# Causal self attention in fp32: in the third and fourth query blocks, four key blocks of a unit are turned by VectorE in 32x32 blocks and moved through DRAM, and their values come last

## The chip, the cores and the metric

The kernel runs on one core of one Trainium2 chip. The metric is the device time of one execution in microseconds. The engines are named as the profile names them: PE is TensorE (PEld its weight loads), DVE VectorE, ACT ScalarE, POOL GpSimd, and SP the engine whose queue issues every DMA of this kernel. Each works through its own instructions in program order; semaphores join them.

## What is computed

An encoder layer over 77 context tokens and a decoder layer over 2 batches of 2048 tokens, width 512, 16 heads of 32, all in fp32. The change is in the decoder's causal self attention:

```python
def _mha(xq, xkv, w_in, b_in, w_out, b_out, bias):
    ...
    scores = jnp.einsum('bhqd,bhkd->bhqk', q, k) / jnp.sqrt(jnp.asarray(hd, xq.dtype))
    scores = scores + bias[None]
    attn = jax.nn.softmax(scores, axis=-1)
    out = jnp.einsum('bhqk,bhkd->bhqd', attn, v)
    out = out.transpose(0, 2, 1, 3).reshape(Bq, Tq, D)
    return out @ w_out.T + b_out
...
causal = jnp.where(jnp.arange(Tt)[None, :] > jnp.arange(Tt)[:, None], -jnp.inf, 0.0)
sb = _rel_bias(dec_rel_self, Tt, Tt) + causal[None]
...
y = y + _mha(yn, yn, dec_sa_in_w, dec_sa_in_b, dec_sa_out_w, dec_sa_out_b, sb)
```

The relative bias is constant beyond 127 tokens, so that only the two key blocks nearest the diagonal need a bias added; a constant for all the other blocks drops out of the softmax.

## The kernel before, in words

The 2048 queries of a batch are four blocks (m = 0 to 3) of 512, each of four tiles (t) of 128. A **unit** (L329) is one batch, block, group g of four heads, and tile: 128 queries by i + 1 = 4m + t + 1 key blocks of 128 by four heads. There are 128 units; the 32 units with m = 2 have 9 to 12 key blocks, and the 32 with m = 3 have 13 to 16. The prediction calls these third-block and fourth-block units. pieces (L315) cuts a unit's key blocks into pieces of at most four.

A unit goes through these steps.

- **scores** (L357): for a piece, four matmuls (L375), one for each head, into four PSUM banks. VectorE evicts each into pp (L384), the SBUF buffer of scores and probabilities, and keeps the maximum; the last piece's two near blocks get their bias on the way (L391). With the unit's last piece VectorE forms nm, the negated maximum (L401). The four exponentials (L406, one for each head, in place, with the sum) are put into a list, late_exps, and issued by ScalarE later (exps, L352).
- **turn** (L412): the values product needs keys on partitions, and pp has queries there. So each 128x128 block of probabilities is transposed by TensorE against the identity (L427): a key block's four heads fill one PSUM bank, a "load", and ScalarE (L434) or VectorE (L432) copies it to a tile of pts. Of eight loads VectorE copies the fifth and the seventh, of fewer the second half.
- **values** (L441): for each key block four matmuls, one for each head, into the four 32-row strips of one bank (L456). The bank is copied to oT (L469), or added to it by VectorE (L471) for a second visit of the unit.

pp holds two units: even units lie at its start, odd ones at its end (probabilities, L344), so that unit n + 2 takes the places of unit n. The eight PSUM banks go round in a ring (bank, L180).

The order around these steps is written out in the loop at L1893. A unit is visited once for each pair of its pieces. A visit issues turn, then (in a unit's last visit) the **slot** of the next unit (L1324: projections, output products, and products of later stages that fill TensorE, with their weight loads into three wqk buffers), then one or two pieces of scores of later units as soon as their places in pp are free (may_score, L1857, score_two, L1873), then values, then more scores. The stream of pieces (L330) runs in order of units and of key blocks.

Softmax sums are inverted, sent through DRAM by SP (rec, rirows: L487, L492) and multiplied into oT by POOL (L494) a slot or two later. SP also loads the bias tiles (L341), the residual rows xr (L262), and the weights (L199, L1038, L1118), and stores y (L1106). A DMA that has to wait holds up all that stand behind it on SP.

## Time and profile before

| What | Time |
|---|---|
| three timed runs | 2726.55, 2729.14, 2731.93 us; median 2729.14 us |
| profiled execution, span from its first to its last instruction | 2726.8 us |
| TensorE busy in that span | 2708.1 us |
| VectorE, ScalarE, GpSimd busy | 1839.9, 1537.0, 1002.4 us |
| DMA, mean of the span | 141 GB/s |

The profile gives the profiled execution's time as its span; what lies around the span is not shown apart, and the span lies within the three runs. Its lines read so: engine, line of the code and operation, output tile <- input tiles, partitions x elements, count; then busy time and mean duration, and the time that the engine stood idle just before these instructions, with what ended most of it. In answers in order of time the first two numbers are start and duration in microseconds, and the idle time before stands in brackets. An fp32 product of scores or values leaves two matmul records, a transpose one.

### The profile page before, as it was taken

How to read it: one execution, taken by the hardware profiler on the slowest of the kernel's cores; microseconds unless marked ns; L12 is line 12 of the kernel's file. 1: busy time of each engine (PE TensorE's matmuls, PEld its weight loads, DVE VectorE, ACT ScalarE, POOL GpSimd, SP SyncE). 2: the span in 40 equal slices, each digit the busy share in tenths (PEclk: the TensorE clock that was granted, in tenths of full speed). 3: DMA queues.
4: the chain of work that ended last, by engine and by line, in shares of the span. 5: the costliest groups of instructions: out<-in, count | busy, mean ns of one | idle time of the engine just before them, and what ended most of it. 6: DMA issues, size and time to landing. Idle time of an engine off the chain costs nothing.

```text
span 2726.8 us, 68267 instructions
## 1 busy us (share of the span) xinstructions
PE 2708.1 (99%) x26606; PEld 2217.9 (81%) x26606; DVE 1839.9 (67%) x5445; ACT 1537.0 (56%) x2978; POOL 1002.4 (37%) x844
## 2 busy tenths in 40 slices
PE   9999999999999999999999999999999999999998
PEld 6678877777876677777777777898989898989898
DVE  4776688888885677788888783646464746464645
ACT  3554567777786547667777784444444444444431
POOL 2612235500300513322300203455556565656456
PEclk9999999999999999999999999999999999999999
DMA  8724355511213522343311206565657565656465
GB/s 242 213 92 135 126 155 164 168 50 43 67 45 89 143 76 72 111 133 98 126 50 35 79 19 220 171 214 173 213 171 239 168 216 170 218 166 219 151 224 185
DMA packets 296277, 385.10 MB, mean 141 GB/s; under 512 B 41184, under 2 KB 165648, under 8 KB 295826
## 3 DMA queue, kind: packets, MB, share of 16 engines
q1 hardware_dynamic: 295954, 380.73, 44.1%
q8 instruction: 211, 3.46, 0.5%
q14 instruction: 112, 0.92, 0.1%
HBM read 334.15 MB, written 46.47 MB: 140 GB/s over the span
## 4 chain that ended last, share of the span: by engine, by line
PE 95%; DVE 1%; ACT 1%; DMA 1%; POOL 1%; issue 1%; SPq 0%; DVEq 0%; POOLq 0%; ACTq 0%
PE psum L427 18%; PE psum L1638 14%; PE psum L1667 13%; PE psum L375 11%; PE psum L456 9%; PE psum L1134 8%; PE psum L1801 3%; PE psum L1758 3%; PE psum L1049 3%; PE psum L866 2%; PE psum L836 1%; PE psum L874 1%; PE psum L590 1%; PE psum L811 1%; PE psum L239 1%; PE psum L215 1%
## 5 line engine op out<-in xcount | busy, mean ns | idle before, releaser
L406 ACT ACTIVATE pp<-pp,nm 128x128 f32<-128x128 f32 (+15 forms) x512 | 611.8, 1200 | 28.6 <-DVE nm L401 27.8
L384 DVE TENSOR_SCALAR_CACHE_REDUCE pp<-psum 128x512 f32<-128x512 f32 (+3 forms) x1024 | 556.2, 591 | 51.3 <-PE psum L375 49.7
L434 ACT COPY pts<-psum 128x512 f32<-128x512 f32 x714 | 384.1, 594 | 312.6 <-PE psum L427 265.6
L427 PE MATMUL psum<-ident,pp 128*128 128x128 f32 x4352 | 530.4, 277 | 4.7 <-ACT nT L310 4.0
L427 PEld LDWEIGHTS psum<-ident,pp 128*128 128x128 f32 x4352 | 474.0, 141 | 55.7 <-DVE pp L384 21.4
L375 PE MATMUL psum<-kT,q 32*128 32x512 f32 (+3 forms) x2560 | 336.5, 559 | 2.5 <-DVE q L217 1.0
L456 PEld LDWEIGHTS psum<-pts,vv 128*32 128x32 f32 x8704 | 226.4, 110 | 127.4 <-DVE pp L384 55.4
L1667 PE MATMUL psum<-pp 128*128 128x128 f32 x2560 | 304.5, 276 | 1.9 <-POOL pp L962 1.6
L1667 PEld LDWEIGHTS psum<-pp 128*128 128x128 f32 x2560 | 296.3, 192 | 8.6 <-issue 2.8
L432 DVE COPY pts<-psum 128x512 f32<-128x512 f32 x374 | 245.2, 685 | 82.6 <-PE psum L427 80.3
L456 PE MATMUL psum<-pts,vv 128*32 128x128 f32 x8704 | 279.6, 276 | 0.8 <-DVE mx L391 0.3
L962 POOL TENSOR_TENSOR pp<-pp 128x512 f32<-128x512 f32 x159 | 212.8, 1356 | 111.0 <-DMA pp<-in_dec_ff_wT_dram 50.6
L1638 PE MATMUL psum<-vv,pp 128*128 128x256 f32 x1024 | 236.2, 381 | 0.0
L375 PEld LDWEIGHTS psum<-kT,q 32*128 32x128 f32 x2560 | 146.3, 183 | 107.1 <-issue 41.3
L1638 PEld LDWEIGHTS psum<-vv,pp 128*128 128x128 f32 x1024 | 190.3, 190 | 25.8 <-issue 0.5
L391 DVE CUSTOM_DVE_ANT_0 pp<-psum,bias 128x256 f32<-128x256 f32 (+1 forms) x512 | 196.0, 411 | 19.7 <-PE psum L375 19.7
L1651 DVE TENSOR_TENSOR kT<-kT,psum 128x512 f32<-128x512 f32 x96 | 65.8, 686 | 191.6 <-PE psum L1638 191.4
L1654 ACT ACTIVATE kT<-kT,vecs 128x256 f32<-128x256 f32 x192 | 86.9, 501 | 156.6 <-DVE kT L1651 155.9
L1638 PE MATMUL psum<-nT,pp 128*128 128x256 f32 x768 | 174.1, 380 | 0.5 <-DVE oT L471 0.5
L1638 PEld LDWEIGHTS psum<-nT,pp 128*128 128x128 f32 x768 | 144.2, 190 | 20.8 <-issue 1.4
L1675 ACT COPY oT<-psum 128x128 f32<-128x128 f32 x56 | 15.0, 268 | 238.9 <-PE psum L1667 238.9
L494 POOL TENSOR_TENSOR oT<-rirows,oT 128x512 f32<-128x512 f32 x30 | 38.4, 1280 | 293.6 <-DMA rirows<-rec 181.7
(272 smaller groups left out, 4110.6 us busy)
## 6 DMA issues: line engine op xcount, KB each, us to landing
pp<-w_d SPq DMA_DIRECT2D x520, 256.0 KB
pp<-in_dec_ff_wT_dram SPq DMA_DIRECT2D x112, 256.0 KB
bias<-tzg SPq DMA_DIRECT2D x128, 128.0 KB
pp<-wo_d SPq DMA_DIRECT2D x56, 256.0 KB
wqk<-in_dec_sa_in_wT_dram SPq DMA_DIRECT2D x52, 256.0 KB
wqk<-sa_q SPq DMA_DIRECT2D x84, 128.0 KB
vv<-in_enc_ff_wT_dram SPq DMA_DIRECT2D x8, 1024.0 KB
xr<-in_x_dram SPq DMA_DIRECT2D x32, 256.0 KB
```

The source lines that it names most:

```text
L375: nc.tensor.matmul(banks[r][:, : kn * P], q[rows4(r), ts(t, P)], kT[rows4(r), g, k0 * P : (k0 + kn) * P], start=True, stop=True,)
L384: nc.vector.tensor_scalar(p[:, k0 : k0 + far], s[:, :far], 1.0, None, ALU.mult, ALU.max, accum_out=st["mx"][:, r, c : c + 1],)
L391: nc.vector.tensor_tensor_reduce(p[:, k0 + far : i + 1], s[:, far:kn], near[:, 2 - (kn - far) :], 1.0, LOWEST, ALU.add, ALU.max, accum_out ...
L406: nc.scalar.activation(p, p, AF.Exp, bias=nm, accum_out=to)
L427: nc.tensor.transpose(pt[:, ts(x, P)], state[n]["p"][r][:, k], ident)
L432: nc.vector.tensor_copy(pts[:, : len(load), :], pt[:, :w])
L434: nc.scalar.copy(pts[:, : len(load), :], pt[:, :w])
L456: nc.tensor.matmul(ot[rows4(r)], vv[:, k, ts(g * HC + r, HD)], got.pop((n, k, r)), start=k == k0 and (whole or not begun), stop=k == k1 - ...
L962: engine.tensor_tensor(out, a, b, ALU.subtract)
L1134: nc.tensor.matmul(mm[:, ts(f, TOK)], left[:, c, ts(f, P)], right[:, c, :], start=c == 0, stop=c == 1,)
L1638: nc.tensor.matmul(mm[:, ts(f, TOK)], a[:, c, ts(f, P)], b[:, c, :], start=fresh and f == 0 and c == 0, stop=c == 1, skip_group_check=True,)
L1667: nc.tensor.matmul(psum[:, bank_i, ts(col, P)], lhs[:, c, :], w[:, c, :], start=fresh and k in (0, 3) and c == 0, stop=c == 3, skip_group_ ...
```

## The change

The first piece of four key blocks (0 to 3, the **far** blocks) of every unit with m = 2 or 3, but for the last two units of all, 62 units together, isn't transposed by TensorE any more.

- Their scores are evicted into pp in another order: within the unit's region of 2048 columns, a 32-key part a of each block, then head, then key block, then the 32 keys. The exponentials are as before.
- At the start of the unit's first visit, move(n) turns the region in place with two VectorE instructions of 128x1024, each of which transposes 32x32 blocks. After each of them SP stores that half (512 KB) to a DRAM tile, turn. Then SP loads the four quarters back, each to 32 partitions (256 KB). Each load waits for both stores.
- The far values are the last products of the unit's last visit. They read the region directly, as the moving operand in four runs of 32 columns, with no copy to pts.
- The pieces of a unit are scored in the order in which they are visited: the far piece last. A place in pp is free once its piece was transposed or, for the far piece, once the far values are issued (held_by, leave). The next user of the region, the far scores of unit n + 2, thus follows unit n's far values.
- A first visit has one piece where m = 2 and two where m = 3; the last visit has the rest.

VectorE in a third-block unit with 12 key blocks, from the sum into oT of the unit before to the inverse of the softmax sums; pp are the probabilities, pts the transposed ones, mx and nm the maxima. Before:

```order
L401 TENSOR_REDUCE nm<-mx 128x4
L471 TENSOR_TENSOR oT<-psum,oT 128x128
L432 COPY pts<-psum 128x512 x2
L384 TENSOR_SCALAR pp,mx<-psum 128x4x128 x8
L432 COPY pts<-psum 128x512 x2
L482 RECIPROCAL ri_109<-sums 128x16
```

The same place now:

```order
L515 TENSOR_TENSOR oT<-psum,oT 128x128
L421 TENSOR_SCALAR pp,mx<-psum 128x4x128 x4
L438 TENSOR_REDUCE nm<-mx 128x4
L385 STREAM_TRANSPOSE pp<-pp 128x1024 x2
L469 COPY pts<-psum 128x512 x2
L421 TENSOR_SCALAR pp,mx<-psum 128x4x128 x4
L469 COPY pts<-psum 128x512 x2
L526 RECIPROCAL ri_111<-sums 128x16
```

The four evictions of the far scores now stand ahead of nm, nm ahead of the two turnings, and these ahead of the copies of the pieces that TensorE still transposes.

TensorE in a fourth-block unit with 15 key blocks, from its first turn; vv are the values, nT and xt operands of the slot. Before:

```order
L427 MATMUL psum<-ident,pp 128x128 x32
L375 MATMUL psum<-kT,q 128x512 x8
L456 MATMUL psum<-pts,vv 32x128 x32
L427 MATMUL psum<-ident,pp 128x128 x28
L1049 MATMUL psum<-nT,wqk 128x256 x2
L1049 MATMUL psum<-xt,wqk 128x256 x2
L375 MATMUL psum<-kT,q 128x256 x4
L375 MATMUL psum<-kT,q 128x384 x4
L456 MATMUL psum<-pts,vv 32x128 x28
L427 MATMUL psum<-ident,pp 128x128 x32
```

The same place now:

```order
L464 MATMUL psum<-ident,pp 128x128 x32
L408 MATMUL psum<-kT,q 128x384 x4
L408 MATMUL psum<-kT,q 128x512 x4
L499 MATMUL psum<-pts,vv 32x128 x32
L464 MATMUL psum<-ident,pp 128x128 x12
L1093 MATMUL psum<-nT,wqk 128x256 x2
L1093 MATMUL psum<-xt,wqk 128x256 x2
L408 MATMUL psum<-kT,q 128x256 x4
L499 MATMUL psum<-pts,vv 32x128 x12
L499 MATMUL psum<-pp,vv 32x128 x16
L408 MATMUL psum<-kT,q 128x512 x4
L464 MATMUL psum<-ident,pp 128x128 x32
```

Sixteen transposes are gone from the second turn, the far values (those from pp) stand at the end, and the far scores of a later unit stand behind them, ahead of the next unit's first turn.

SP in two units of batch 0's fourth block, from the bias loads; xr are residual rows, y the stored result, turn the DRAM tiles. Before:

```order
L341 DMA bias<-tzg_76 32x4x256 x4
L199 DMA wqk<-in_dec_sa_in_wT_dram 128x4x128
L262 DMA xr<-in_x_dram 128x512 x2
L1106 DMA y_0_2_79<-xr 128x512 x2
L492 DMA rirows<-rec_114 32x512 x4
```

The same place now:

```order
L355 DMA bias<-tzg_76 32x4x256 x4
L199 DMA wqk<-in_dec_sa_in_wT_dram 128x4x128
L262 DMA xr<-in_x_dram 128x512 x2
L386 DMA turn_109<-pp 128x2x512 x2
L388 DMA pp<-turn_109 32x4x512 x4
L1150 DMA y_0_2_79<-xr 128x512 x2
L536 DMA rirows<-rec_116 32x512 x4
L386 DMA turn_110<-pp 128x2x512 x2
L388 DMA pp<-turn_110 32x4x512 x4
L199 DMA wqk<-in_dec_sa_in_wT_dram 128x4x128
```

Each unit puts two stores and four loads into SP's queue, between the loads and stores of the slots.

The diff, cut to its core:

```diff
         units = [(b, m, g, t) for b in range(B) for m in range(NMB) for g in range(NC) for t in range(TB)]
-        stream = [(n, k0, kn) for n, u in enumerate(units) for k0, kn in pieces(u[1] * TB + u[3])]
+
+        def moved(n):
+
+            return units[n][1] >= 2 and n < len(units) - 2
+
+        def visits_of(n):
+
+            ps = pieces(units[n][1] * TB + units[n][3])
+            if not moved(n):
+                return [(ps[v : v + 2], []) for v in range(0, len(ps), 2)]
+            far, *ps = ps
+            first = 2 if units[n][1] == NMB - 1 else 1
+            return [(ps[:first], []), (ps[first:], [far])]
+
+        stream = [(n, *p) for n in range(len(units)) for v in visits_of(n) for p in v[0] + v[1]]
         state = {}
         biases = {}
 
...
 
             for _ in range(min(k, len(late_exps))):
                 late_exps.pop(0)[1]()
+
+        bounce = [dram.tile([RB // 8, P, HC * P], F32, name=f"turn{k}", tag=f"turn{k}") for k in range(2)]
+
+        def region(n):
+
+            w = (units[n][1] + 1) * MB
+            at = END - HC * w if n % 2 else 0
+            return pp[:, at : at + HC * MB]
+
+        def move(n):
+
+            area = region(n).rearrange("p (a c) -> p a c", a=HC)
+            to = bounce[n // 2 % 2]
+            for a in (0, 2):
+                two = region(n)[:, a * HC * P : (a + 2) * HC * P]
+                nc.vector.transpose(two, two)
+                nc.sync.dma_start(to[a : a + 2].rearrange("a p c -> p a c"), area[:, a : a + 2])
+            for a in range(HC):
+                nc.sync.dma_start(area[rows4(a)], to[a].rearrange("(a q) c -> q a c", q=RB))
 
         def scores(n, k0, kn):
             b, m, g, t = units[n]
...
             for r in range(HC):
                 p, s, c = st["p"][r], banks[r].rearrange("p (k x) -> p k x", x=P), col
                 if far:
+                    to, got_s = p[:, k0 : k0 + far], s[:, :far]
+                    if k0 == 0 and moved(n):
+                        to = to.rearrange("p a (k x) -> p a k x", x=RB)
+                        got_s = got_s.rearrange("p k (a x) -> p a k x", x=RB)
                     nc.vector.tensor_scalar(
-                        p[:, k0 : k0 + far], s[:, :far], 1.0, None, ALU.mult, ALU.max,
+                        to, got_s, 1.0, None, ALU.mult, ALU.max,
                         accum_out=st["mx"][:, r, c : c + 1],
                     )
                     c += 1
...
 
         sums_held = {}
 
-        def values(pair):
-            n, k0, _ = pair[0]
+        def values(n, turned, far, ends):
             b, m, g, t = units[n]
-            i = m * TB + t
-            k1 = pair[-1][1] + pair[-1][2]
+            for k0, kn in far:
+                parts = region(n).rearrange("p (a r k x) -> p r k a x", a=HC, r=HC, x=RB)
+                for k in range(kn):
+                    for r in range(HC):
+                        got[n, k0 + k, r] = parts[:, r, k]
+            ks = [k for k0, kn in turned + far for k in range(k0, k0 + kn)]
+            opens = not turned or turned[0] == visits_of(n)[0][0][0]
             whole = m == 0
             key = (b, m, g) if whole else n
             begun = key in sums_held
...
                 sums_held[key] = ring.pop(0)
             v = sums_held[key]
             ot = psum[:, v, ts(t, P)] if whole else psum[:, v, :P]
-            keep = t < TB - 1 if whole else (g, t) == (2, 0) and k1 <= i
-            for k in range(k0, k1):
+            keep = t < TB - 1 if whole else (g, t) == (2, 0) and not ends
+            for k in ks:
                 for r in range(HC):
+                    p = got.pop((n, k, r))
+                    o = ot[rows4(r)]
                     nc.tensor.matmul(
-                        ot[rows4(r)], vv[:, k, ts(g * HC + r, HD)], got.pop((n, k, r)),
-                        start=k == k0 and (whole or not begun), stop=k == k1 - 1 and (whole or not keep),
+                        o if len(p.shape) == 2 else o.rearrange("p (a x) -> p a x", x=RB),
+                        vv[:, k, ts(g * HC + r, HD)], p,
+                        start=k == ks[0] and (whole or not begun), stop=k == ks[-1] and (whole or not keep),
                     )
             if keep:
                 return
...
             o = ots[b, m, g]
             if whole:
                 nc.scalar.copy(o, psum[:, v, :])
-            elif k0 == 0 or begun:
+            elif opens or begun:
                 nc.scalar.copy(o[:, ts(t, P)], ot)
             else:
                 nc.vector.tensor_tensor(o[:, ts(t, P)], ot, o[:, ts(t, P)], ALU.add)
...
+        def places(n, k0, kn):
+
+            w = (units[n][1] + 1) * MB
+            k0 += (END - HC * w) // (HC * P) if n % 2 else 0
+            return range(k0, k0 + kn)
+
+        def may_score(ahead=0):
+
+            if at[0] + ahead >= len(stream):
                 return False
-            n, k0, kn = stream[at[0]]
-            if n < 2:
-                return True
-            moved = TB * max(0, units[n - 2][1] - units[n][1]) if n % 2 else 0
-            return turned_to[n - 2] >= min(k0 + kn + moved, size[n - 2])
+            n = stream[at[0] + ahead][0]
+            return not any(k in held_by for k in places(*stream[at[0] + ahead])) and (
+                n < 2 or units[n][1] == units[n - 2][1] or turned_all[n - 2]
+            )
+
+        turned_all = {n: False for n in range(end)}
+
+        def score_at(ahead=0):
+            n, k0, kn = stream[at[0] + ahead]
+            scores(n, k0, kn)
+            scored_to[n] += kn
+            held_by.update({k: n for k in places(n, k0, kn)})
...
+        def leave(n, ps):
+            for p in ps:
+                for k in places(n, *p):
+                    assert held_by.pop(k) == n
+
         score_next()
         score_next()
         slot(0)
-        i = 0
-        while i < len(stream):
-            n = stream[i][0]
-            pair = [p for p in stream[i : i + 2] if p[0] == n]
-            while scored_to.get(n) != size[n]:
+        for n, visit, turned, far in ((n, k, *w) for n in range(end) for k, w in enumerate(visits_of(n))):
+            pair = [(n, *p) for p in turned]
+            while scored_to[n] != size[n]:
                 score_next()
             while any(u == n for u, _ in late_exps):
                 exps(1)
-            ends = pair[-1][1] + pair[-1][2] == size[n]
+            ends = visit == len(visits_of(n)) - 1
+            if moved(n) and visit == 0:
+                move(n)
             turn(pair)
             if n == end - 2:
                 for _, k0, _ in pair:
                     feed(k0 + 4)
-            turned_to[n] = pair[-1][1] + pair[-1][2]
+            leave(n, turned)
+            turned_all[n] = ends and not far
             third = units[n][1] == 2
             if third and ends:
                 exps(2)
...
                     score_next()
             if third and not ends:
                 exps(1)
-            values(pair)
-            while may_score() and (len(pair) > 1 or units[n][1] == 0):
+            values(n, turned, far, ends)
+            leave(n, far)
+            turned_all[n] = ends
+            while may_score() and (len(pair) > 1 or units[n][1] == 0 or far):
                 score_next()
             if third and not ends:
                 exps(1)
-            i += len(pair)
```

20 lines of the change are left out of this document (7 added, 13 removed).

## The prediction

> **What bounds the kernel now.** The page's head and busy shares come first, then the busy time of each engine in the stages that the change touches. The stages are cut at the first exponential of each block: in batch 0 the third block's units start near 362 us, the fourth's near 578 us, and the last one ends near 845 us.
>
> ```profile
> span 2726.8 us, 68267 instructions
> PE 2708.1 (99%) x26606; PEld 2217.9 (81%) x26606; DVE 1839.9 (67%) x5445; ACT 1537.0 (56%) x2978; POOL 1002.4 (37%) x844
> ```
>
> ```profile
> 361.72 1.26 ACT L406 ACTIVATE pp<-pp,nm 128x1152 f32<-128x1152 f32 x1
> 577.94 1.69 ACT L406 ACTIVATE pp<-pp,nm 128x1664 f32<-128x1664 f32 x1
> ```
>
> ```profile
> core 0: us, PE busy (x) PEld busy (x) DVE busy (x) ACT busy (x) POOL busy (x), PEclk, DMA share, GB/s
> 362.00:578.00 216.00, 215.90 (x2605) 167.93 (x2606) 177.53 (x606) 157.37 (x275) 92.34 (x77) 1.00 0.49 149
> 578.00:845.00 267.00, 266.55 (x3478) 209.65 (x3471) 212.40 (x707) 210.72 (x326) 30.81 (x24) 1.00 0.15 48
> 1176.00:1392.00 216.00, 215.91 (x2600) 168.03 (x2598) 177.58 (x609) 157.23 (x274) 58.40 (x46) 1.00 0.34 109
> 1392.00:1655.00 263.00, 262.16 (x3531) 209.89 (x3531) 213.65 (x698) 204.25 (x305) 24.07 (x19) 1.00 0.20 64
> ```
>
> Each row is 16 units. TensorE is busy for all of a stage but a microsecond, so it sets the pace: 216/16 = 13.5 us for a third-block unit, (267+263)/32 = 16.56 us for a fourth-block one. VectorE is busy 11.1 us and 13.3 us of these. DMA is half idle or more.
>
> Next, what a transpose is worth. The grouped row has its total; the order of time shows 32 of them in a row, then eight score products, and when VectorE can start on these.
>
> ```profile
> L427 PE MATMUL psum<-ident,pp 128*128 128x128 f32 x4352 | 530.4, 277 | 4.7 <-ACT nT L310 4.0
> ```
>
> ```profile
> 478.10 1.08 PE L456 MATMUL psum<-pts,vv 128*32 128x128 f32 x32
> 660.24 3.71 PE L427 MATMUL psum<-ident,pp 128*128 128x128 f32 x32
> 663.88 2.00 PE L375 MATMUL psum<-kT,q 32*128 32x512 f32 x16
> 665.04 0.69 DVE L384 TENSOR_SCALAR_CACHE_REDUCE pp<-psum 128x512 f32<-128x512 f32 x1 [0.80 <-PE psum L375]
> 672.40 0.28 DVE L384 TENSOR_SCALAR_CACHE_REDUCE pp<-psum 128x128 f32<-128x128 f32 x1
> 674.06 0.69 DVE L384 TENSOR_SCALAR_CACHE_REDUCE pp<-psum 128x512 f32<-128x512 f32 x1
> 676.62 0.17 DVE L401 TENSOR_REDUCE nm<-mx 128x4 f32<-128x20 f32 x1
> 676.91 1.28 DVE L432 COPY pts<-psum 128x512 f32<-128x512 f32 x2
> ```
>
> The 32 transposes take 3.71 us and a single one 0.27, so they follow each other at (3.71-0.27)/31 = 0.111 us. A score product or a value product has two records each in these rows, so x16 is two pieces of scores (1.0 us a piece) and x32 is the values of four key blocks (1.05 us).
>
> **The change part by part.** *Removed:* 16 transposes in each of 62 units (64 from the third block on, less the last two), 992 x 0.111 = 110 us of TensorE, or 1.78 us a unit; and 248 evictions, most of them ScalarE's, which nothing on the path waits for. If nothing took its place the kernel would end at 2617 us.
>
> *Added on VectorE:* two 32x32 turnings of 128x1024 per unit. The trace has only a small one, and a copy that runs faster than the others:
>
> ```profile
> L484 DVE STREAM_TRANSPOSE rt<-ri x30: 211/211/214, 52.7 to 1535.6; 128x32 f32<-128x32 f32 x30
> L503 DVE COPY rirows<-ri x2: 427/428/429, 1598.8 to 1653.9; 128x512 f32<-128x512 f32 x2
> ```
>
> From 128 to 512 columns an eviction goes from 0.28 to 0.69 us, 1.07 ns a column. At that rate a turning is 0.211 + 992 x 1.07 ns = 1.27 us, two 2.5 us. The low end is the rate of the copy from SBUF, 0.428 us for 512 columns where the eviction takes 0.69: about half, 0.73 us each. The high end is two cycles a column, 2.3 us, which the 211 ns row doesn't exclude, since it is mostly fixed cost. I take 1.27, because the row of its own operation fits it with no assumption. [...] No run here shows a large one yet.
>
> VectorE's work in a unit is then 11.1 - 0.3 + 2.5 = 13.3 us (third block) and 13.3 - 0.6 + 2.5 = 15.2 us (fourth), against 11.7 and 14.8 us left on TensorE. Already by sums VectorE becomes the fuller engine.
>
> *Where it stands.* In the order VectorE turns unit n+1 straight after it evicted the far scores of unit n+2 and formed nm, and ahead of the copies of the turned pieces; and these far scores come only after unit n's far values, which wait for its four reads. That makes two chains that each close once per unit.
>
> *Chain A, through DRAM:* far values 1.05; scores to first eviction 665.04-663.88 = 1.16; four evictions and nm 676.62+0.17-674.06 = 2.73; two turnings 2.5; writes; reads; then far values of the next unit. The trace has no such round trip, so writes and reads are bounded by these rows:
>
> ```profile
> 2723.27 0.81 SPq L1695 DMA_DIRECT2D out_dram<-vv  x2
> 2724.00:2725.50 1.50, 0.00 (x0) 0.00 (x0) 0.00 (x0) 0.00 (x0) 0.00 (x0) 0.50 0.92 347
> ```
>
> ```profile
> 459.86 1.96 SPq L978 DMA_DIRECT2D pp<-in_dec_ca_in_wT_dram  x4
> 476.69 1.21 SPq L262 DMA_DIRECT2D xr<-in_x_dram  x2
> 479.59 1.28 POOL L1104 TENSOR_TENSOR xr<-xr,row_dec_sa_out_b 128x512 f32<-128x512 f32 x1 [0.18 <-DMA xr<-in_x_dram]
> 799.00:801.00 2.00, 2.00 (x20) 1.58 (x21) 1.38 (x2) 1.53 (x4) 0.64 (x1) 1.00 1.04 392
> ```
>
> The kernel's last two stores, 0.5 MB like the second write, are issued at 2723.27 and moving until 2725.5, and the span ends at 2726.8: 2.2 to 3.5 us. I take 3.4, since the reads need the landing and not the last byte. (The first write runs beside the second turning.) A load of 256 KB is used 479.59-476.69 = 2.9 us after its issue; the reads move 768 KB more, 2.0 us at 392 GB/s or 2.4 us at 320: 4.9 to 5.3 us, and four issues take 1.96 us within that. I take 5.1. Quickest ends 2.2 + 4.0 = 6.2 us, where the reads overlap fully; slowest 3.5 + 7 = 10.5 us, behind the third block's own 149 and 109 GB/s. Chain A: 1.05 + 1.16 + 2.73 + 2.5 + 3.4 + 5.1 = 16.0 us.
>
> [...]
>
> *Chain B, through the copies:* in a fourth-block unit TensorE's second score piece needs the banks of two transposes that VectorE copies (1.28 us) behind the turnings. It is through 1.16 + 2.73 + 2.5 + 1.28 + about 1.0 = 8.7 us after the far scores began. In that time TensorE has only far scores 1.0, 31 transposes 3.5 and two pieces 2.0 = 6.5 us. It waits 2.2 us where it gained 1.78: 16.56 - 1.78 + 2.1 = 16.9 us (2.1 because its last product overlaps). In a third-block unit the values of the turned pieces wait for the two copies until 7.7 us, with 4.2 us of work before: 13.5 - 1.78 + 3.5 = 15.2 us.
>
> *Sum.* Third block: the later chain is A, 16.0 - 13.5 = +2.5 us in 32 units, +80. Fourth block: the later is B, 16.9 - 16.56 = +0.34 in 30 units, +10. 2726.8 + 90 = 2817 us of span; the median of the runs is 2.3 us above that span, so 2819.
>
> *Costed at nothing.* SP stands from the first write until the reads are out, some 6 us, with weight loads, bias loads, the stores of y and the rows of sums queued behind.
>
> ```profile
> SPq L1118 <- PE psum L1134: 343.1, 56, 15.8
> ```
>
> These loads already wait for TensorE to free a buffer, up to 15.8 us, and are used a slot or more later; their cover is that lead. If it is gone TensorE waits for weights, up to about 3 us in a unit with a slot's load behind a move, some +30 in all. The score evictions now write (and read PSUM) in runs of 32: 0 by the 128-to-512 row, in which four runs cost what their columns do; if they cost, it is on both chains, 0.3 us a unit. Reading the moving operand in four runs of 32: 0, nothing in the trace prices it.
>
> **The rivals.** *Faster.* The turning runs at the rate of the SBUF copy, 0.73 us, and the second score piece gets its banks one copy earlier. Chain B in the fourth block then waits 2.1 - 1.1 - 0.9 = 0.1 us: -1.66 x 30 = -50; the third block, with the round trip at its quick end, is held by chain B at 14.1 us: +0.6 x 32 = +19. Together -31, 2698 us. It decides at a turning below about 1.0 us. For it speaks L503, against it the row of the turning itself. Chance 0.12.
>
> *No change.* The change works, but the round trip is 6.2 us and the values of the third block begin before the copies: +0.2 x 32 against -0.2 x 30, 2729 us. Chance 0.07.
>
> *Much slower.* Two cycles a column: +2.1 us on both chains, 62 units: +130, 2949 us. Chance 0.10.
>
> *Slower still by the clock.* The trace shows a lower granted clock where TensorE pauses:
>
> ```profile
> 2718.00:2726.80 8.80, 3.39 (x31) 3.20 (x29) 2.16 (x5) 0.12 (x1) 0.00 (x0) 0.82 0.33 121
> ```
>
> A third-block unit would idle 16.0 - 11.7 = 4.3 us in two pauses. If one of them drops the clock, the 2.1 us of far values and scores behind it, which lie on chain A, take up to twice as long: +1.5 x 32 = +48, 2867 us. [...] Chance 0.07.
>
> *Forecast,* slower by the two chains: 0.64.
>
> **How the numbers follow.** About 0.2% (5 us) is what a measurement of this kernel can tell from no change. Slower: 0.64 + 0.10 + 0.07 = 0.81; same 0.07; faster 0.12. The range runs from 2710, round trip at its quick end with part of the fast turning, to 2895, round trip at its slow end (+2.0 x 32 over the forecast) with the clock's share; the fast and the much slower case lie outside, with a little less than 0.2.
>
> **What would show it.** The changed profile should have 992 fewer L427-type transposes and about 2600 us of TensorE; TensorE idle before the far values, waiting for the reads, in the third block; idle before the fourth block's second score piece or the values, waiting for VectorE's copies; units of about 16.0 and 16.9 us; a large turning of 1.27 us; 8.5 us from the second turning's end to the far values. Wrong if TensorE stays 99% busy with a span near 2620 to 2700, if the turning is near 0.7 or 2.3 us, if the reads are in before TensorE comes to the far values in the third block, or if the time goes to weight loads or a lower clock.

## The result, and the profile after

The changed kernel takes 3036.53 us, the median of four runs (3029.84 to 3037.21), against 2728.38 us for the kernel before beside it: a ratio of 1.1121, 95% interval 1.1105 to 1.1137. The forecast was 2819 us with a range up to 2895. The direction was right, and the size was missed by 217 us.

Head, busy shares and granted clock of the page of the profile:

```profile
span 3034.4 us, 66826 instructions
PE 2772.2 (91%) x25614; PEld 2172.5 (72%) x25614; DVE 1951.1 (64%) x5523; ACT 1439.2 (47%) x2776; POOL 1000.7 (33%) x844
PEclk9999998888999999998888999899999999999999
```

The span is 307.6 us longer. TensorE has 992 matmul records fewer and is yet 64 us longer busy; its idle time went from 18.7 to 262.2 us. The granted clock falls in the slices of the third and fourth blocks, in both batches. The same stages as before, cut at the first exponential of each block:

```profile
core 0: us, PE busy (x) PEld busy (x) DVE busy (x) ACT busy (x) POOL busy (x), PEclk, DMA share, GB/s
362.50:668.40 305.90, 237.27 (x2358) 162.90 (x2356) 206.03 (x628) 130.11 (x220) 92.05 (x77) 0.88 0.72 207
668.40:984.10 315.70, 268.64 (x3180) 188.00 (x3184) 240.57 (x727) 189.16 (x276) 30.79 (x24) 0.94 0.52 149
1320.90:1625.00 304.10, 238.08 (x2340) 163.89 (x2339) 206.19 (x628) 130.30 (x220) 58.46 (x47) 0.87 0.61 180
```

A third-block unit now takes 305.9/16 = 19.1 us (before 13.5, forecast 16.0), a fourth-block one 19.7 (16.56, forecast 16.9). No engine is full in them. TensorE's longest waits (us in total, times, longest):

```profile
PE psum L499 <- DMA pp<-turn: 104.5, 39, 6.3
PE psum L499 <- DVE pts L469: 76.2, 76, 3.6
PE psum L1178 <- DMA wqk<-in_dec_sa_in_wT_dram: 26.5, 4, 6.8
PE psum L408 <- DVE pts L469: 21.8, 19, 1.6
PE psum L1093 <- DMA wqk<-sa_q: 4.7, 2, 2.5
```

The far values wait for the loads, the near values and some score products (L408) for copies, and some 31 us go to late weights. One move in order of time, VectorE, SP (SyncE) and TensorE:

```profile
775.64 0.17 DVE L438 TENSOR_REDUCE nm<-mx 128x4 f32<-128x16 f32 x1
775.72 2.36 DVE L385 STREAM_TRANSPOSE pp<-pp 128x1024 f32<-128x1024 f32 x2
778.01 1.85 DVE L469 COPY pts<-psum 128x512 f32<-128x512 f32 x3
```

```profile
776.99 1.88 SPq L386 DMA_DIRECT2D turn<-pp  x2
781.73 2.50 SPq L388 DMA_DIRECT2D pp<-turn  x4
```

```profile
783.41 0.64 PE L499 MATMUL psum<-pts,vv 128*32 128x128 f32 x16
788.89 1.93 PE L499 MATMUL psum<-pp,vv 128*32 128x128 f32 x32 [4.84 <-DMA pp<-turn]
```

The turnings end at 778.08, the loads are issued at 781.73 when both stores are in (3.65 us), and the far values begin at 788.89 (7.16 us). The copies stand right behind the turnings. And the far values, behind a pause of 4.84 us, take 1.93 us where four key blocks took 1.05 before; the granted clock is 0.50 in the windows from 789 to 791.

This move is one of the longer ones. Over all 62 moves the median from the end of the turnings to the loads' issue is 3.2 us, and from there to the far values it is 7.0 us in the 42 units in which TensorE stood idle for more than 0.3 us before them; in the other 20 the loads were in, or nearly so, when TensorE came. An earlier move, in the third block, shows a round with little disturbance, from one unit's far values to the next unit's:

```profile
449.30 1.08 PE L499 MATMUL psum<-pp,vv 128*32 128x128 f32 x32
454.12 2.36 DVE L385 STREAM_TRANSPOSE pp<-pp 128x1024 f32<-128x1024 f32 x2
459.89 1.75 SPq L388 DMA_DIRECT2D pp<-turn  x4
466.53 1.08 PE L499 MATMUL psum<-pp,vv 128*32 128x128 f32 x32 [3.20 <-DMA pp<-turn]
```

It takes 17.2 us. The median of the 58 rounds between moved units of one stage is 18.7 us, the least 16.9.

### The profile page after: what moved, and what is told of

It reads as the page before. It is cut to its first block, busy times and chain, and to the rows that moved or that the text cites. A ratio compares the mean times of both kernels' runs of the same rounds, so it can differ in the third digit from the quotient of the medians.

```text
span 3034.4 us, 66826 instructions
## 1 busy us (share of the span) xinstructions
PE 2772.2 (91%) x25614; PEld 2172.5 (72%) x25614; DVE 1951.1 (64%) x5523; ACT 1439.2 (47%) x2776; POOL 1000.7 (33%) x844
## 4 chain that ended last, share of the span: by engine, by line
PE 65%; DMA 16%; DVE 14%; SPq 2%; issue 1%; POOL 1%; ACT 1%; DVEq 0%; POOLq 0%; ACTq 0%
PE psum L1682 13%; PE psum L1711 11%; DMA pp<-turn 8%; DVE pp L421 7%; PE psum L408 6%; PE psum L464 6%; PE psum L499 5%; PE psum L1178 5%; DMA turn<-pp 5%; DVE pp L385 5%; PE psum L1845 3%; PE psum L1802 3%; SPq L388 2%; PE psum L910 2%; PE psum L1093 2%
## 5 line engine op out<-in xcount | busy, mean ns | idle before, releaser
L471 ACT COPY pts<-psum 128x512 f32<-128x512 f32 x512 | 278.0, 590 | 619.3 <-PE psum L464 527.7
L464 PEld LDWEIGHTS psum<-ident,pp 128*128 128x128 f32 x3360 | 396.7, 150 | 102.9 <-issue 41.1
L464 PE MATMUL psum<-ident,pp 128*128 128x128 f32 x3360 | 454.4, 292 | 4.6 <-ACT nT L310 4.0
L408 PE MATMUL psum<-kT,q 32*128 32x512 f32 (+3 forms) x2560 | 409.7, 608 | 24.3 <-DVE pts L469 21.8
L499 PEld LDWEIGHTS psum<-pts,vv 128*32 128x32 f32 x6720 | 170.9, 111 | 212.4 <-DVE pts L469 99.1
L499 PE MATMUL psum<-pts,vv 128*32 128x128 f32 x6720 | 249.3, 283 | 77.1 <-DVE pts L469 76.2
L408 PEld LDWEIGHTS psum<-kT,q 32*128 32x128 f32 x2560 | 155.3, 195 | 162.9 <-issue 60.8
L469 DVE COPY pts<-psum 128x512 f32<-128x512 f32 x328 | 212.0, 677 | 82.3 <-PE psum L464 79.7
L499 PE MATMUL psum<-pp,vv 128*32 128x128 f32 x1984 | 81.3, 314 | 112.6 <-DMA pp<-turn 104.5
## 6 DMA issues: line engine op xcount, KB each, us to landing
pp<-w_d SPq DMA_DIRECT2D x520, 256.0 KB
pp<-turn SPq DMA_DIRECT2D x248, 256.0 KB
pp<-in_dec_ff_wT_dram SPq DMA_DIRECT2D x112, 256.0 KB
pp<-wo_d SPq DMA_DIRECT2D x56, 256.0 KB
wqk<-in_dec_sa_in_wT_dram SPq DMA_DIRECT2D x52, 256.0 KB
```

The source lines that it names most:

```text
L408: nc.tensor.matmul(banks[r][:, : kn * P], q[rows4(r), ts(t, P)], kT[rows4(r), g, k0 * P : (k0 + kn) * P], start=True, stop=True,)
L464: nc.tensor.transpose(pt[:, ts(x, P)], state[n]["p"][r][:, k], ident)
L469: nc.vector.tensor_copy(pts[:, : len(load), :], pt[:, :w])
L471: nc.scalar.copy(pts[:, : len(load), :], pt[:, :w])
L499: nc.tensor.matmul(o if len(p.shape) == 2 else o.rearrange("p (a x) -> p a x", x=RB), vv[:, k, ts(g * HC + r, HD)], p, start=k == ks[0] an ...
```

## The experiments

Two theories stood at the start: *clock* (pauses halve TensorE's clock, and this stretches everything) and *transfer* (the loads are longer than forecast, the clock is a symptom), beside the forecast's own two chains. Each stage column is the length of a stage of 16 units in batch 0. Where the fourth blocks alone are moved the third-block stage is left out, as are the stages of the runs with loads from four rows.

| kernel | us | ratio to before, 95% interval | third | fourth | clock |
|---|---|---|---|---|---|
| before | 2728.4 | | 216.2 | 264.7 | 0.997 |
| changed | 3036.5 | 1.1105–1.1137 | 305.9 | 315.7 | 0.957 |
| order only | 2717.0 | 0.9947–0.9974 | 220.0 | 248.1 | 0.991 |
| turnings, no trip | 2862.2 | 1.0466–1.0501 | 264.0 | 276.3 | 0.973 |
| trip, no turnings | 2804.0 | 1.0257–1.0299 | 272.5 | 255.9 | 0.974 |
| turnings, no trip, copies on ScalarE | 2745.3 | 1.0040–1.0074 | 227.8 | 256.0 | 0.987 |
| order only, copies on ScalarE | 2736.6 | 1.0018–1.0038 | 225.9 | 253.1 | 0.988 |
| changed, copies on ScalarE | 3073.3 | 1.1239–1.1276 | 324.7 | 323.4 | 0.940 |
| changed, 4.55 us of filler | 3192.0 | 1.1675–1.1710 | 349.4 | 359.1 | 0.972 |
| no trip, 1.37 us of filler | 2827.0 | 1.0338–1.0378 | 245.3 | 279.7 | 0.985 |
| changed, 1.37 us of filler twice | 3041.0 | 1.1123–1.1157 | 311.5 | 322.9 | 0.975 |
| move a visit earlier | 3021.7 | 1.1056–1.1089 | 325.6 | 306.9 | 0.956 |
| fourth only, turnings at the slot | 2848.3 | 1.0419–1.0450 | | 319.7 | 0.973 |
| fourth only, turnings at the values | 2785.8 | 1.0192–1.0223 | | 285.6 | 0.989 |
| narrow stores, wide loads | 3141.8 | 1.1497–1.1535 | 338.2 | 346.8 | 0.940 |
| loads from four rows | 3546.0 | 1.2973–1.3011 | | | 0.895 |
| the same, copies on ScalarE | 3559.3 | 1.3020–1.3063 | | | 0.880 |
| the same, fourth only | 3093.5 | 1.1317–1.1351 | | | 0.937 |
| loads on two queues | 3073.5 | 1.1246–1.1284 | 334.1 | 317.2 | 0.951 |
| two queues, fourth only, copies on ScalarE | 2859.7 | 1.0460–1.0505 | | 312.2 | 0.977 |

### The change taken apart

Without stores and loads:

```diff
-                nc.sync.dma_start(to[a : a + 2].rearrange("a p c -> p a c"), area[:, a : a + 2])
-            for a in range(HC):
-                nc.sync.dma_start(area[rows4(a)], to[a].rearrange("(a q) c -> q a c", q=RB))
```

> The changed kernel without the stores and loads through DRAM: the turnings and the order stay, the far values take what lies in the buffer after the turning alone (so the moving of blocks between partitions is left out of what is computed). Clock theory and transfer theory: the pauses of TensorE ahead of the far values go and the half clock with them; what is left is the wait for copies behind the turnings, by the forecast 15.2 us a third-block unit and 16.9 a fourth-block one, so 2720 to 2800 us at a granted clock of 0.985 or more. Rival (VectorE's turnings ahead of the copies are what costs): the waits for copies stay at over 2 us a unit and the time stays above 2930 us.

Measured 2862.2 us. It lies between the two ranges: with the turnings in place the trip is worth 174 us, and 145 of what is left come with the turnings, as the next run shows, which takes these out too.

```diff
-                nc.vector.transpose(two, two)
```

> As the kernel without stores and loads, and without the turnings too: the far values take the probabilities as they lie in the buffer (the turning of these four key blocks is left out of what is computed). What is left of the change is its order, the evictions in runs of 32 and 992 transposes fewer. If the order and the strided evictions cost nothing: 2729 less 110, 2610 to 2650 us, granted clock 0.99 or more. If the later scores alone make TensorE wait (rival: the order is the cost): over 2730 us.

Measured 2717.0 us, between the two ranges again: of the 110 us that 992 transposes weigh, 12 show. The fourth-block stages gain 16.6 us each, the third-block ones lose 4. TensorE in a third-block unit, before and here:

```profile
450.10 3.71 PE L427 MATMUL psum<-ident,pp 128*128 128x128 f32 x32
453.74 1.87 PE L375 MATMUL psum<-kT,q 32*128 32x384 f32 x16
```

```profile
451.65 1.14 PE L404 MATMUL psum<-kT,q 32*128 32x512 f32 x8
452.72 1.97 PE L460 MATMUL psum<-ident,pp 128*128 128x128 f32 x16
454.62 2.39 PE L404 MATMUL psum<-kT,q 32*128 32x384 f32 x8
```

The far scores come later in the unit, and the next scores follow after 1.97 us instead of 3.71, so VectorE is still evicting and the four products of a piece start one by one as banks come free: 2.39 us for one piece where two took 1.87. Over the kernel the score products are busy 391.8 us instead of 336.5, and TensorE's idle time is 48.9 us (2714.0 - 2665.1) instead of 18.7. I read it so: the transposes had been the time in which VectorE evicted scores. No run tests this reading by itself.

The third part, the trip without the turnings (the diff is that of the turnings alone):

> The changed kernel without the turnings; stores and loads stay, so blocks are moved between partitions but not turned (that is left out of what is computed). Theory (chains): the chain through DRAM is 2.44 us shorter, 15.8 us a unit, and no copy stands behind a turning: third-block stages 250 to 265 us, fourth-block ones 250 to 262, 2780 to 2840 us. Rival (the trip costs its 174 us whatever else is there, added to the 2717 us without turnings and trip): 2870 to 2910 us.

Measured 2804.0 us. That is within the theory's range, but partly by luck, since the edit does more than the theory says. The turnings hold the stores back until VectorE has evicted the far scores of a later unit; without them they wait for the exponentials. What SP's stores wait for, in the changed kernel and here:

```profile
SPq L386 <- DVE pp L385: 549.6, 120, 17.3
SPq L385 <- ACT pp L442: 89.3, 27, 10.9
```

In the changed kernel the first store of a move is issued 6.5 us (median) after the far values of the unit before began, here at the moment when they begin. So this run takes the stores out of the chain that closes once per unit, and TensorE waits for the loads 40.1 us in 18 places, not 104.5 in 39. Against the order alone a trip that may start so early costs 87 us, and a trip behind the turnings 174. Turnings cost 145 us without the trip and 233 with it, and the second figure holds the place that they force on the stores. The costs don't add. (The table has batch 0; in batch 1 the third blocks of this run take 244.3 us instead of 272.5.)

### The copies behind the turnings

```diff
-                if free or (o % 2 if first else o in (4, 6) if len(loads) == 8 else o >= (len(loads) + 1) // 2):
+                if free or not moved(load[0][0]) and (o % 2 if first else o in (4, 6) if len(loads) == 8 else o >= (len(loads) + 1) // 2):
```

> The kernel without stores and loads (the moving of blocks between partitions left out) at 2862 us, and in it all copies of turned probabilities of the moved units on ScalarE, so that none stands behind a turning on VectorE. Theory (copies stand in VectorE's queue behind the turnings, TensorE waits 76 us for them in 74 pauses, and the pauses lower its clock): the waits for copies go, the third-block stages fall from 264 us towards 220 to 230 and the fourth-block ones from 276 towards 250 to 258; 2740 to 2780 us, granted clock 0.985 or more. Rival (VectorE's turnings delay the scores' evictions, and so PSUM banks, just as much): 2820 us or more, with waits for evictions in place of those for copies.

> No turnings, no stores and loads (both left out of what is computed), and all copies of the moved units on ScalarE: the order of the change and its 992 transposes fewer, with VectorE relieved. Against 2745 us with the turnings, the difference is what 2.44 us of turnings a unit cost when no copy stands behind them. If evictions queued on VectorE were what kept the removed 110 us from showing (2717 instead of about 2620): 2650 to 2690 us. If it was the order of TensorE's own steps: within 10 us of 2717; if ScalarE's copies now wait behind the exponentials: over 2717.

> The changed kernel, whole, with all copies of the moved units on ScalarE. Without the trip this took 117 us off, since no copy stood behind a turning any more. Theory (two chains of about equal length: the one through DRAM, far values 1.06, scores 1.14, evictions 2.73, turnings 2.44, stores 3.65, loads 7.16 us, makes 18.2 us a unit by itself): the chain through DRAM still sets the unit, third-block stages stay at 285 us or more, 2950 to 3030 us in all. Rival (the copies are the cost here too and the trip only adds to what they wait): the same 117 us go, 2900 to 2930 us.

Without the trip: 2745.3 us, so 117 of the turnings' 145 us go when no copy stands behind them in VectorE's queue. The same kernel without the turnings takes 2736.6 us, so that the turnings by themselves cost 9 us once the copies are elsewhere. The row of order before and after it, in the kernel without trip:

```profile
454.06 2.36 DVE L385 STREAM_TRANSPOSE pp<-pp 128x1024 f32<-128x1024 f32 x2
456.34 1.25 DVE L466 COPY pts<-psum 128x512 f32<-128x512 f32 x2
```

```profile
457.05 0.42 PE L496 MATMUL psum<-pts,vv 128*32 128x128 f32 x8 [1.36 <-DVE pts L466]
```

Without turnings the same edit costs 20 us (2736.6 against 2717.0). The expectation put such a cost on ScalarE's copies, which then stand behind its exponentials; the trace doesn't show that apart. Relieving VectorE of copies did not bring the missing 98 us back. With the trip the edit gives nothing and costs 37 us, more than its range allowed, while TensorE's wait for the loads grows from 104.5 to 165.8 us. This speaks for the chain through DRAM as what sets the unit whatever the copies do. Why it got worse than unchanged was not settled.

### The clock

80 matmuls of zeros between near and far values (the later fillers have 24):

```diff
+                if far and k == far[0][0]:
+                    for x in range(80):
+                        nc.tensor.matmul(ot[rows4(x % HC)], nought, ident, start=False, stop=False)
```

> The changed kernel with 80 further matmuls of zeros (32 columns of weights, 128 moving) between a moved unit's near values and its far values, where TensorE waits for the transfer; they add zero to the sums. At the 33 ns that a value takes (32 in 1.06 us) they are 2.66 us in each of 62 units, 165 us in all, on an engine that is already the bound. Clock theory (a pause of TensorE longer than about 1.3 us is followed by some microseconds of half clock, which costs 174 us of busy time and stretches the steps of the path that run on TensorE): the work fills the pauses, the mean granted clock rises from 0.957 to 0.98 or more and the time falls, in spite of the added work, to 2880 to 2970 us. Transfer theory (reads of 7.2 us instead of 5.1 make the units longer and the clock is only a symptom): the filler stands in place of the waits and the time stays within 1% of 3036 us, or is longer by up to 60 us where no wait covers it.

Measured 3192.0 us, outside both ranges, since I sized it wrongly: one such matmul is two records, and the 80 took 4.55 us, not 2.66. The wait for the loads went from 104.5 to 3.3 us and the third-block clock from 0.88 to 0.92; added work of 290 us cost 156. As a test of the theories it tells little. The next filler fits the pause it fills, ahead of the third near block, in the kernel without trip:

> The kernel without stores and loads (moving left out) at 2862 us, and in it 24 matmuls of zeros (48 records, 1.37 us at the 28 ns a record took in the first filler) in each third-block unit at the place where TensorE waits 1.4 to 1.6 us for a copy behind the turnings; they add zero. If the half clock that follows such pauses costs time: the pauses end, the granted clock of the third-block stages rises from 0.90 to 0.97 or more, and 20 to 50 us go in spite of the work added. If the unit is set by VectorE's chain and the slow clock only fills time in which TensorE would wait: the clock rises as much, and the time stays within 10 us of 2862.

Measured 2827.0 us. Sixteen fillers a stage, and the stage is shorter by 18.7 us, its clock 0.99 for 0.90 (the row of the kernel without filler first):

```profile
361.90:625.90 264.00, 230.30 (x2337) 162.10 (x2336) 205.44 (x627) 129.73 (x218) 91.74 (x77) 0.90 0.41 122
```

```profile
360.60:605.90 245.30, 231.07 (x3103) 165.56 (x3106) 204.48 (x628) 129.51 (x219) 92.89 (x78) 0.99 0.44 132
```

So half clock costs time in the kernel without trip: 35 us in all. In the whole changed kernel, with the filler at both places:

> The changed kernel with 24 matmuls of zeros (1.37 us) in each moved unit ahead of the far values, and as many in each third-block unit where TensorE waits for copies behind the turnings: the first filler with a third of its length. 62 times 1.37 and 30 times 1.37 make 126 us of added work. If half clock after pauses costs time in the whole kernel: granted clock 0.97 or more (0.957 without) and a time of 2950 to 3015 us. If the chain through DRAM sets the unit whatever the clock: the time stays within 15 us of 3037 or rises by up to 40.

3041.0 us: the clock rose from 0.957 to 0.975 and the time did not fall. This speaks for the chain through DRAM; that a gain by the clock and a cost of the filler of the same size met there isn't excluded.

### Where the turnings stand

The move of unit n+1 in the last visit of unit n, then the same idea on the fourth blocks alone with turnings and transfers placed apart, at the slot or behind the values (the diff is the core of the first):

```diff
+            early = ends and n + 1 < end and moved(n + 1) and scored_to[n + 1] == size[n + 1]
+            while early and any(u == n + 1 for u, _ in late_exps):
+                exps(1)
             turn(pair)
+            if early:
+                move(n + 1)
```

> The changed kernel with the move of unit n+1 (turnings, stores, loads) put into the last visit of unit n, behind its copies and ahead of the far scores' evictions, with the exponentials of unit n+1 drawn ahead of it and two DRAM buffers taken in turn by every unit. Each trip has a whole unit's time to land, and the chain far values, scores, eviction, turning, trip closes over two units instead of one. Clock theory and transfer theory: the waits for the trip nearly go, the granted clock is 0.985 or more, 2660 to 2780 us. Rival (the exponentials drawn ahead on ScalarE and the turnings delay the copies just as much): over 2850 us.

> Only the fourth blocks moved; the turnings of unit n+1 stand in the last visit of unit n behind the projections' slot, the stores and loads behind that unit's last scores, two DRAM buffers in turn, and the copies of the last visit on ScalarE (VectorE keeps two of the first eight). The turning needs no step of TensorE's unit n any more, and the trip has most of a unit. If the chain through DRAM was the cost and VectorE has room (203 us of copies and evictions, 39 of turnings and 25 less of copies in a stage of about 250): the two fourth-block stages take 250 to 262 us instead of 264.7, 2700 to 2730 us, granted clock 0.985 or more. Rival (2.4 us of turnings ahead of evictions keep TensorE waiting wherever they stand): the stages take 275 us or more, 2750 to 2790 us.

> As the one before, with the turnings of unit n+1 behind the values of unit n and the evictions of its first scores, ahead of the evictions of the far scores. If the place of 2.4 us on VectorE decides, it differs from the one before by 10 us or more; if the trip's length does, it is slower (the trip starts about 3 us later), 2710 to 2760 us; if neither, the two are within 5 us.

The first gave 3021.7 us, so the rival's side, though mostly by other means than it named. The trip is early enough: no wait of the far values for it is among TensorE's longest. TensorE waits for weights instead, and SyncE's queue stands for up to 27.7 us at the stores, until the turnings (L385) are through:

```profile
SPq L386 <- DVE pp L385: 521.7, 91, 27.7
PE psum L1178 <- DMA wqk<-in_dec_sa_in_wT_dram: 62.7, 6, 15.3
PE psum L1093 <- DMA wqk<-sa_q: 45.1, 7, 10.7
```

The second gave stages of 319.7 us, worse than with the move where the change has it (315.7): TensorE waits 33.5 us for score banks whose evictions stand behind the turnings, and the turnings wait 62.5 us for exponentials:

```profile
PE psum L412 <- DVE mx L432: 33.5, 19, 4.2
...
DVE pp L383 <- ACT pp L447: 62.5, 25, 5.1
```

The third gave 285.6 us and 2785.8 in all, 2.1% slower than before (interval 1.9 to 2.2). It is the fastest of the kernels that compute everything. The place of the turnings, together with that of the exponentials drawn ahead of them, decides by 34 us a stage; in none of the places tried did they cost nothing.

### The loads

First the shuffle put into the stores: four stores from 32 partitions, two loads into 128.

```diff
-                nc.sync.dma_start(to[a : a + 2].rearrange("a p c -> p a c"), area[:, a : a + 2])
             for a in range(HC):
-                nc.sync.dma_start(area[rows4(a)], to[a].rearrange("(a q) c -> q a c", q=RB))
+                nc.sync.dma_start(to[a].rearrange("(a q) c -> q a c", q=RB), area[rows4(a)])
+            for a in (0, 2):
+                nc.sync.dma_start(area[:, a : a + 2], to[a : a + 2].rearrange("a p c -> p a c"))
```

> The changed kernel with the shuffle in the stores instead of the loads: four stores of 256 KB from 32 partitions each, behind both turnings, and two loads of 512 KB into 128 partitions. The same bytes and the same runs of 2 KB. If the reads took 7.2 us instead of the forecast 5.1 because each went into 32 partitions: the reads fall to about 4 us and the writes grow to 5 to 7, the trip is about as long and the time within 40 us of 3036. If reads from DRAM are slower than writes whatever their shape: reads stay at 6 to 7 us, writes at 3.4 to 4. If only 32-partition loads are slow and stores are not: the trip falls from 10.8 to 7.5 us and the time by 60 us or more.

3141.8 us, so 105 longer, not within 40. Both rates turned round with the shape: from the loads' issue to waiting far values it is now 5.3 us in the median, not 7.0, and from the turnings' end to the loads' issue 6.3, not 3.2. The rows are narrow loads in the changed kernel, then narrow stores and wide loads here:

```profile
785.00:787.00 2.00, 0.00 (x0) 0.00 (x0) 0.85 (x4) 0.09 (x1) 0.00 (x0) 1.00 0.95 233
```

```profile
804.00:809.00 5.00, 4.67 (x82) 3.41 (x83) 5.00 (x15) 2.93 (x6) 0.00 (x0) 1.00 0.85 200
811.00:815.00 4.00, 3.95 (x51) 2.81 (x49) 2.92 (x10) 2.02 (x4) 3.64 (x3) 1.00 0.98 344
```

In these windows what goes to or from 32 partitions moves at 200 to 233 GB/s with the DMA engines busy, and the wide transfer at 344. The narrow stores can only start behind both turnings, where the first wide store ran beside the second turning; the wait for the trip grew from 104.5 to 181.4 us.

Then loads that fill 128 partitions from four separate rows, alone, with copies on ScalarE, and on fourth blocks alone:

```diff
             for a in range(HC):
-                nc.sync.dma_start(area[rows4(a)], to[a].rearrange("(a q) c -> q a c", q=RB))
+                nc.sync.dma_start(area[:, a], to[:, ts(a, RB)])
```

> The changed kernel with loads that fill all 128 partitions with 512 columns each (64 KB from each of four places of the DRAM buffer), in place of loads into 32 partitions; the stores stay wide, the same bytes, the same result. Theory (the loads took 7.2 us instead of the forecast 5.1 because each went into 32 partitions): loads take 3.7 to 4.3 us, the chain through DRAM falls from 18.2 to about 15 us, and the chain through copies, which does not change, holds the stages where they were without any trip: third blocks 264 to 275 us, fourth 276 to 285, 2860 to 2910 us. Rival (reads from DRAM are slow whatever their shape): loads stay at 6 us or more and the time at 2990 us or more.

> As the one before, and all copies of the moved units on ScalarE: both chains shortened at once. Alone, the copies gave nothing here (3073 us). Theory of two chains: third-block stages 235 to 250 us, fourth-block ones 256 to 262, 2760 to 2810 us. Rival (the chain through DRAM still sets it): 2850 us or more.

> Only the fourth blocks moved, with wide loads and their copies on ScalarE; the third blocks as before the change. Theory: a chain through DRAM of 15 us is within the 15.5 to 16.5 us of a fourth-block unit, so the two stages take what they took without a trip, 256 to 260 us instead of 264.7: 2710 to 2722 us, faster than before by 0.2 to 0.7%. Rival (a trip of 8 us still ends late in most units): stages of 268 us or more, 2735 us or more.

All three failed for one reason (3546.0, 3559.3 and 3093.5 us), so the theory was not tested: loads of this form took longer than narrow ones. From the loads' issue to the far values it is 14.4 to 14.5 us in the median of each of the three, not 7.0. In the first of them:

```profile
807.00:811.00 4.00, 0.00 (x0) 0.00 (x0) 0.00 (x0) 0.00 (x0) 0.00 (x0) 0.50 0.26 102
```

A DMA share of 0.26 and 102 GB/s, where the narrow loads of the changed kernel had 0.95 and 233. Why the share is so low no run shows.

Last, two of the four narrow loads on GpSimd's queue:

```diff
-            for a in range(HC):
-                nc.sync.dma_start(area[rows4(a)], to[a].rearrange("(a q) c -> q a c", q=RB))
+            for a in (0, 2, 1, 3):
+                (nc.gpsimd if a >= 2 else nc.sync).dma_start(area[rows4(a)], to[a].rearrange("(a q) c -> q a c", q=RB))
```

> The changed kernel with two of a move's four loads (partitions 64 to 127) issued by GpSimd on its own queue beside SyncE's two (partitions 0 to 63), same shape, same bytes. Theory (four loads in one queue go into the same 32 partitions at a time, 230 GB/s, where loads into 128 partitions reached 370 to 410): two loads run side by side, the loads take 4 to 5.5 us instead of 7.2, the chain through DRAM falls from 18.2 to 15.5 to 16.5 us and the chain through copies takes over: third-block stages 265 to 285 us, fourth 276 to 290, 2860 to 2950 us. Rival (the loads are no faster, or GpSimd, standing behind the stores, brings the weights late): 2990 us or more.

> Only the fourth blocks moved, two loads on GpSimd's queue and two on SyncE's, and the copies of the moved units on ScalarE. Theory of two chains: a chain through DRAM of 15.5 to 16.5 us is about a fourth-block unit (16.56 before, 14.8 without its transposes), so the stages take 256 to 268 us instead of 264.7: 2710 to 2740 us, at best faster than before by 0.6%. Rival (the trip still ends late in most units): stages of 275 us or more, 2750 us or more.

3073.5 and 2859.7 us, the rivals' side in both. Two queues side by side were hardly faster than one (loads of the first run):

```profile
707.00:713.00 6.00, 4.68 (x50) 3.71 (x48) 2.25 (x6) 1.32 (x3) 0.61 (x2) 1.00 1.02 244
```

Six microseconds at 244 GB/s, share 1.02, where one queue had 233 at 0.95 and the wide loads 344 at 0.98.

## Why the prediction was right in direction and wrong in size

**Right.** A turning took 1.22 us (forecast 1.27, with both other ends out), the stores 3.65 us in the move shown and 3.2 in the median (3.4). The order of the steps, and that TensorE would wait at the far values for loads and at the near ones for copies, is in the waits. The rivals *faster*, *no change* and *much slower* each had a condition (0.73 us, a trip of 6.2 us, 2.3 us) that did not come. Two signs that the text itself named as showing it wrong did come: time in weight loads, and a lower clock. (Its two cases outside the range have chances of 0.12 and 0.10, together 0.22 and not less than 0.2.)

```profile
L385 DVE STREAM_TRANSPOSE pp<-pp 128x1024 f32<-128x1024 f32 x124 | 146.4, 1219 | 0.0
```

**The first step that failed: "I take 5.1" for the reads.** They take 7.16 us in the move shown and 7.0 in the median where TensorE waits. The upper rate of 392 GB/s came from a row of loads into 128 partitions, and no row showed the lower one of 320; these loads go into 32 partitions at a time, at 233. The upper end (7) was near it, and the text had no row for the shape.

**The second follows: "the later chain is A, 16.0" and "Fourth block: the later is B".** With the terms of the move shown first, chain A is 1.06 + 1.14 + 2.73 + 2.44 + 3.65 + 7.16 = 18.2 us, the figure that the expectations use. With the medians, and 2.36 for two turnings in a row, it is 1.06 + 1.14 + 2.73 + 2.36 + 3.17 + 7.03 = 17.5, beside 17.2 in the round shown. Chain B was sized fairly: the run with turnings and no trip shows it, 264.0/16 = 16.5 us (forecast 15.2; with the filler 245.3/16 = 15.3) and 276.3/16 = 17.3 (16.9). So chain A is the longer one in the third block, and in the fourth the two are about equal: TensorE waited for the loads in 22 of 32 third-block units and in 20 of 30 fourth-block ones. The sum with 17.5: (17.5 - 13.5) x 32 + (17.5 - 16.56) x 30 = +128 + 28, where I had +90. The longer chain A makes 66 of the 217 us that the forecast missed.

**The third: costed at nothing, the weights.** Waits of 26.5 + 4.7 us; the text had "some +30" if the cover goes, and its price was right.

**The fourth: the clock, chance 0.07.** It came. In half-microsecond windows from 362 to 984 us TensorE pauses 55 times. Of 19 pauses below 1.25 us none is followed by half clock, of 14 from 1.25 to 2 us seven are, of 16 up to 4 us ten, and all six longer ones. The stretches at half clock last 3.4 us or a multiple of it, 109 us in all. Length alone doesn't decide: in the trace's record of the granted clock the starts of all 57 stretches of the kernel lie within 0.02 us of one grid of 3.413 us, and how busy TensorE was between two points of it tells more. Of the steps of the grid at full clock in which it was busy for less than 45%, all 36 were followed by half clock; of those with 45 to 62%, 16 of 37; of the busier ones, 4 of 739 (the two bounds are read off these counts). So by these counts a pause of 1.4 us was followed by half clock or not, depending on where it fell on the grid and what else was idle there. Three pauses in windows of 1 us (the second figure is TensorE's busy time; the last three are the granted clock, the DMA share and GB/s):

```profile
496.00:497.00 1.00, 0.14 (x8) 0.00 (x0) 1.00 (x1) 1.00 (x3) 0.00 (x0) 1.00 0.09 35
497.00:498.00 1.00, 0.28 (x8) 0.16 (x8) 1.00 (x3) 1.00 (x3) 0.00 (x0) 1.00 1.01 369
498.00:499.00 1.00, 0.83 (x18) 0.45 (x11) 1.00 (x4) 1.00 (x2) 0.00 (x0) 0.79 1.01 389
499.00:500.00 1.00, 1.00 (x6) 1.00 (x6) 1.00 (x5) 1.00 (x4) 0.00 (x0) 0.50 0.69 256
...
911.00:912.00 1.00, 0.32 (x4) 0.00 (x0) 1.00 (x2) 1.00 (x1) 0.00 (x0) 1.00 0.56 211
912.00:913.00 1.00, 0.73 (x6) 0.43 (x8) 1.00 (x3) 1.00 (x3) 0.00 (x0) 1.00 1.04 381
914.00:915.00 1.00, 1.00 (x40) 1.00 (x44) 1.00 (x5) 0.21 (x2) 0.00 (x0) 1.00 0.30 96
...
936.00:937.00 1.00, 0.00 (x0) 0.00 (x0) 1.00 (x3) 0.86 (x2) 0.00 (x0) 1.00 1.05 221
939.00:940.00 1.00, 0.00 (x0) 0.00 (x0) 0.00 (x0) 0.00 (x0) 0.00 (x0) 0.50 0.86 232
944.00:945.00 1.00, 1.00 (x8) 0.00 (x0) 1.00 (x9) 0.00 (x0) 0.00 (x0) 0.50 0.00 0
```

After 1.75 us of idle time from 496 on the clock is 0.50 in the window at 499; after 0.95 us from 911 on it stays at 1.00; in the pause from 935 to 940 it drops at 939, and it is still 0.50 at 944. How long a pause has to be was not shown by any row that the forecast had, and its small chance was an estimate; here half of the 14 pauses from 1.25 to 2 us were enough. Two batches make at most some 110 us of TensorE's time lost at half clock; with 55 us of score products spread out by banks, that is up to 165 of the 174 us by which its busy time exceeds the forecast's 2598. But busy time is not the span. Where the chain through DRAM waits for a transfer anyway, half clock may cost nothing, as the run with both fillers suggests (clock 0.975 for 0.957, 3041.0 us for 3036.5). On the chain itself stand the far values (81.3 us against 66.4 in the run with the order alone) and the scores (409.7 against 391.8): 33 us, an estimate, since not every score product is on the chain.

**The whole.** Added up from these terms, 2726.8 + 128 + 28 (chain) + 31 (weights) + 33 (slow clock on the chain) = 2947 of 3034.4 us; no run shows that they add, and the other 87 us are not assigned. The rounds say where the time lies. The 58 rounds between moved units of one stage take 237 of the 308 us (the forecast had 85 there): 135 because an undisturbed round is 17.3 us long (4.8 from the far values to the next turning, 2.4, 3.1 and 7.0), and 102 because many are longer. Of the 102, 65 lie between the far values and the next turning; in 29 rounds this step is longer than 4.9 us, and in 21 of these half clock fell into it. Another 16 lie in the stores and 21 between the loads' issue and the far values. The 71 us outside these rounds are not taken apart.

The forecast's "if nothing took its place", 2617 us, was wrong as well, by about 98 us: the order alone ends at 2717, as I read it because TensorE's transposes were the cover of VectorE's evictions (55 us are in the score products, 30 in idle time). This stayed hidden in the sum, since the chains were compared with the unit before and not with the work left.

No version that computes everything beats the kernel before. Even with a trip that costs nothing and no copy behind a turning the kernel takes 2745.3 us, 0.4 to 0.7% more than before; by its stages the fourth blocks would gain 8.7 us each and the third ones lose 11.6.

## What to carry to other kernels

Add up the whole ring of steps that comes back to its own start once per unit, with a measured price for the shape of each transfer, and compare it with the unit: here 17.5 us against 13.5 in the third block, and no engine was full. An instruction in an engine's queue can put a transfer on that ring: the turnings cost 9 us by themselves, but they held the stores behind another unit's evictions. A step taken off the fullest engine is worth its time only if nothing used that time as cover: look for what the next engine did meanwhile. And pauses of some 1.5 us on TensorE were not free in the kernel without trip; where such a wait must stay, work that fills it can pay (35 us there, nothing in the whole kernel).

## What the runs showed of the hardware beside

- Transfers to or from 32 partitions ran at 200 to 244 GB/s with a DMA share of 0.85 to 1.02, on one queue or two; to or from 128 partitions at 330 (stores in the run with two queues, share 0.88) and 344 (loads in the run with narrow stores, share 0.98).
- A load from four separate rows of DRAM ran at 102 GB/s with a DMA share of 0.26.
- Half clock began on a grid of 3.413 us (57 stretches, within 0.02 us) and lasted one step or more. It came after all 36 steps in which TensorE was busy less than 45%, after 16 of 37 with 45 to 62%, and after 4 of 739 busier ones; of the 14 pauses from 1.25 to 2 us seven were followed by it.
- A 32x32 turning of 128x1024 in place took 1.22 us (124 of them, 1.201 to 1.236), 1.19 ns a column.
